# Two-step graph layer with top-p attention: slots of one row tile, PE's work interleaved by hand, proofs tested once a step

## The chip, the cores and the metric

The kernel runs on one core of a Trainium2 chip. Its engines work side by side, each through its own list of instructions in order: TensorE (PE in the profile; PEld is its weight loads), VectorE (DVE), ScalarE (ACT), GpSimd (POOL) and SyncE (SP), which here only issues transfers. The metric is device microseconds (us) of one execution of the whole program, as the median of several runs.

## The reference, cut to what matters

```python
def attention(X):                       # top-p attention, TOP_P = 0.9
    q = X @ W1.T @ W2.T                 # 64 wide
    k = X @ W3.T
    probs = softmax(q @ k.T, axis=-1)
    # per row: keep the largest entries until their sum reaches 0.9
    ...
    A = probs * mask
    return A / A.sum(-1)

h = relu(layernorm(x))                  # x is 3327 x 256
R = adj + eye; R = R / R.sum(-1)
Xf = Xa = h; Z = 0
for n in range(2):
    A = attention(Xa)
    Xf = R @ Xf
    Xa = A @ Xa
    Z = Z + Xf @ U1[n].T + Xa @ U2[n].T
out = x + layernorm(h + Z) * ln_g + ln_b
```

Everything is in 32-bit floats. The hard part is the mask: each row of 3327 exponentials has to be cut at the value where the largest ones first hold 90% of the row's sum.

## The kernel before, in words

The 3327 rows are padded to 3328, that is 26 row tiles (NT) of 128 rows. There are two functions. `guess_graph_layer` does the work with a guessed cut for every row and proves the guess; if a proof fails for any row, a flag is set, and `tile_graph_layer` (line 713) then runs `search_graph_layer`, which finds every cut by bisection. In the trace only the first one runs.

Ahead of the steps, a loop over the tiles takes the layernorm of x and calls `prep`, which makes keys and queries of a tile. Each of the two steps then runs over the row tiles, and a tile t goes through these stages:

- `weights` (from line 446): the query is projected (pq, lines 450 and 451), all 3328 logits of the tile are made on PE (pl, line 473), and ACT takes the exponentials (e, lines 477 to 482) with their sums. Then POOL works through a string of 128x1 instructions (lines 483 to 511): from the row's sum Z and the moments of its logits it guesses a threshold, column 9, and the bias column 10 for ACT.
- `first` (from line 516): ACT passes over e twice, with Relu (line 520) and Sign (line 522), and so finds the mass and the count above the guess. A string on POOL (lines 523 to 529) corrects the guess.
- `second` (from line 532): DVE passes over e once more (jv, line 536) for the mass below the corrected guess, and POOL corrects again (lines 538 to 563) and gives column 16.
- `settle` (from line 566): DVE blanks everything above column 16 (w, line 571) and sums it, finds the eight largest of each of 20 segments (cand, line 576), takes the 48 largest of these in six rounds of eight (lines 581 and 583), and finds among them the exact cut. It then cuts e in place (line 594). Seven instructions on POOL (lines 599 to 605) test whether the cut is proven, and add to the flag.
- `attend` (from line 608): PE transposes the cut e in groups of four 128x128 blocks (pt, line 614), ACT copies each group to SBUF (eT, line 616), and PE multiplies with the node values (pa, line 618). DVE takes the reciprocal of the row sum (ra, line 621), and ACT scales (xa, line 622).
- `prep` of the new values in step 0, `finish` in step 1 (from line 642): finish multiplies the four parts with U1 and U2 (pz, line 648), adds, normalises (y, lines 651 to 658) and stores (line 660). pa and pz share one PSUM buffer.
- `diffuse` (from line 625), called by `spread` (line 673): the product with the adjacency (pr, line 632), whose blocks `at` come by six transfers on SP (line 630) into three buffers. DVE adds the identity (line 638) and POOL scales (line 639).

The driver loop at the end of the function writes, for slot i: settle(i), second(i+1), attend and prep or finish of i-1, weights(i+3), first(i+2), spread(i). This is the order in which the instructions are traced. The Tile framework lays them out on each engine by itself: earlier traced ones have priority, but one that its own estimate finds ready goes ahead of one that waits. So the order on an engine need not be the traced one; in the trace, pr matmuls of spread, which is traced last, run between the groups of attend. The waits between engines come from the data.

Of the kernel before, what the change touches and what calls it, by code (L numbers as in the profile page):

```python
# [9 lines left out]
F32 = mybir.dt.float32  # L10
# [8 lines left out]
P = 128  # L19
# [304 lines left out]
def guess_graph_layer(ctx, tc, x, adj, w1t, w2t, w3t, u1t, u2t, ln_g, ln_b, out, flag):  # L324
# [9 lines left out]
    small = ctx.enter_context(tc.tile_pool(name="small", bufs=6))  # L334
# [53 lines left out]
    qm = const.tile([P, 2, 2 * DA + 1], F32, tag="qm", name="qm")  # L388
# [48 lines left out]
    def moments(step):  # L437
# [5 lines left out]
        V.tensor_copy(qm[:, step, DA:], pq[:, 0, : DA + 1])  # L443


    def weights(step, t):
# [4 lines left out]
        PE.matmul(pq[:, 1:3, :].rearrange("p a b -> p (a b)")[:, : 2 * DA + 1], qry[qp, j, :],  # L451
                  qm[qp, step, :], start=True, stop=True)
        qT = tpool.tile([P, P], F32, tag="qT", name="qT", bufs=2)
        S.copy(qT, pq[:, 0, :])
        r = {}
        mq = small.tile([P, 2], F32, tag="mq", name="mq")
        qj = small.tile([P, DA], F32, tag="qj", name="qj", bufs=1)
        pr_ = pq[:, 1:3, :].rearrange("p a b -> p (a b)")
        V.tensor_copy(mq[:, 0:1], pr_[:, 2 * DA : 2 * DA + 1])
        qs = small.tile([P, DA], F32, tag="qs", name="qs", bufs=2)  # L460
        V.tensor_copy(qs, pr_[:, :DA])
        V.scalar_tensor_tensor(qj, qs, 1.0, pr_[:, DA : 2 * DA], ALU.mult, ALU.mult,
                               accum_out=mq[:, 1:2])
        e = epool.tile([P, NP], F32, tag="e", name="e")
        za = small.tile([P, 4], F32, tag="za", name="za")
        G.memset(e[:, N:NP], 0.0)
        w = HALF * P
        for n, c in enumerate(range(0, w, 512)):
# [7 lines left out]
            if wd == 512:  # L476
                S.activation(e.rearrange("p (a n) -> p a n", a=2)[:, :, c : c + wd], pl[:, :, :wd],  # L477
                             AF.Exp, accum_out=za[:, n : n + 1])
            else:
                zb = small.tile([P, 1], F32, tag="zb", name="zb")  # L480
                S.activation(e[:, c : c + wd], pl[:, 0, :wd], AF.Exp, accum_out=zb)
                S.activation(e[:, w + c : N], pl[:, 1, : wd - 1], AF.Exp, accum_out=za[:, n : n + 1])
                G.tensor_tensor(za[:, n : n + 1], za[:, n : n + 1], zb, ALU.add)

        g = small.tile([P, 24], F32, tag="g", name="g")
        col = lambda k: g[:, k : k + 1]
        m = mq[:, 0:1]
        G.tensor_tensor(g[:, 5:7], za[:, 0:2], za[:, 2:4], ALU.add)
        G.tensor_tensor(col(0), col(5), col(6), ALU.add)
        G.tensor_tensor(col(1), col(0), pwr[:, 5:6], ALU.pow)  # L490
        G.tensor_scalar(col(1), col(1), 10.0, None, ALU.mult)
        G.tensor_scalar(col(2), m, m, mq[:, 1:2], ALU.mult, ALU.subtract)
# [261 lines left out]
```

## Time and profile before

| | |
|---|---|
| median of 3 runs | 3013.88 us (3010.37 to 3015.91) |
| the profiled execution | 3012.75 us |
| its span, from first to last instruction | 3010.9 us |
| mean granted clock of TensorE | 0.826 |
| PE busy | 2023.4 us, 67% of the span |
| POOL busy | 1538.8 us, 51% |
| DVE busy | 1188.7 us, 39% |
| ACT busy | 841.3 us, 28% |

Busy time is the time in which at least one instruction of the engine runs; matmuls are pipelined, so a busy PE is not PE at its peak. A wait is listed as: engine, tile and line that waited, then what released it, with the sum in us, the number of times and the longest. In rows in order of time stand the start, the duration, the engine, the line, the operation, out<-in, shapes and the count; in brackets the idle time before it and what ended that.

### The profile page before, as it was taken

The numbers are of one execution on the slowest core, as the hardware profiler recorded it, in microseconds if no ns is written. First come the engines' busy times: TensorE is split into PE (matmuls) and PEld (weight loads), VectorE is DVE, ScalarE is ACT, GpSimd is POOL, SyncE is SP. The second block draws the span as 40 slices with busy tenths as digits, with TensorE's granted clock in tenths as the row PEclk, the third lists the DMA queues.
The fourth block names the chain that finished last, engine by engine and source line by source line (L and its number), as shares of the span: only waits on it lengthen the run. The fifth ranks groups of instructions, "written<-read, shape, count | busy, mean of one in ns | idle before, by whom it ended". The sixth has DMA issues, their size and how long they took to land.

```text
span 3010.9 us, 28189 instructions
## 1 busy us (share of the span) xinstructions
PE 2023.4 (67%) x9055; PEld 1557.0 (52%) x9055; DVE 1188.7 (39%) x3075; ACT 841.3 (28%) x1536; POOL 1538.8 (51%) x3711
## 2 busy tenths in 40 slices
PE   7846666666766666778846567666676767576778
PEld 5534444445545454556634445455554545454566
DVE  2145544443535343442045534433433353334330
ACT  4422323223232323222332232222223222322221
POOL 4375655555454545553186655455455545554531
PEclk9968777787878888888977878887888878888889
DMA  4110000000001101111110010111011011101111
GB/s 127 56 36 28 19 23 15 19 23 23 23 20 30 36 29 37 32 37 46 38 41 21 26 31 27 31 44 31 27 36 39 26 31 40 35 26 31 40 40 38
DMA packets 58605, 102.31 MB, mean 34 GB/s; under 512 B 7249, under 2 KB 25168, under 8 KB 58448
## 3 DMA queue, kind: packets, MB, share of 16 engines
q1 hardware_dynamic: 55936, 98.85, 11.3%
q10 hardware_dynamic: 2512, 1.57, 0.2%
q8 instruction: 73, 1.20, 0.2%
q14 instruction: 84, 0.69, 0.1%
HBM read 96.99 MB, written 3.41 MB: 33 GB/s over the span
## 4 chain that ended last, share of the span: by engine, by line
POOL 43%; PE 18%; DVE 16%; ACT 11%; issue 10%; DMA 2%; SPq 0%; ACTq 0%; POOLq 0%; DVEq 0%
PE pr L632 6%; DVE w L571 6%; POOL g L552 6%; ACT ja L522 5%; DVE cand L576 4%; PE pz L648 4%; ACT ja L520 4%; POOL f L600 3%; PE pa L618 2%; DVE cand L583 2%; DVE bb L581 2%; DMA xr<-in_x 1%; POOL g L504 1%; PE pk L423 1%; PE pt L412 1%
## 5 line engine op out<-in xcount | busy, mean ns | idle before, releaser
L618 PE MATMUL pa<-xa,eT 128*128 128x257 f32 x1352 | 374.3, 434 | 246.7 <-ACT eT L616 246.7
L618 PE MATMUL pa<-x,eT 128*128 128x257 f32 x1352 | 371.0, 432 | 246.4 <-ACT eT L616 246.3
L536 DVE SCALAR_TENSOR_TENSOR jv<-e,g 128x3328 f32<-128x3328 f32 x52 | 191.7, 3686 | 754.4 <-POOL g L529 754.4
L618 PEld LDWEIGHTS pa<-xa,eT 128*128 128x128 f32 x1352 | 286.0, 218 | 322.9 <-ACT eT L616 275.3
L618 PEld LDWEIGHTS pa<-x,eT 128*128 128x128 f32 x1352 | 287.4, 218 | 318.0 <-ACT eT L616 268.7
L632 PE MATMUL pr<-xf,at 128*128 128x256 f32 x1352 | 346.7, 396 | 73.8 <-DVE xf L638 39.1
L632 PE MATMUL pr<-x,at 128*128 128x257 f32 x1352 | 371.2, 409 | 1.5 <-DMA at<-in_adj 0.9
L616 ACT COPY eT<-pt 128x512 f32<-128x512 f32 (+1 forms) x364 | 186.2, 554 | 647.1 <-PE pt L614 646.9
L571 DVE SCALAR_TENSOR_TENSOR w<-e,g 128x3328 f32<-128x3328 f32 x52 | 192.2, 3697 | 435.1 <-POOL g L563 412.3
L520 ACT ACTIVATE ja<-e,g 128x3328 uint8<-128x3328 f32 x52 | 159.5, 3067 | 703.9 <-POOL g L508 703.9
L632 PEld LDWEIGHTS pr<-xf,at 128*128 128x128 f32 x1352 | 248.4, 196 | 121.5 <-DMA at<-in_adj 41.6
L632 PEld LDWEIGHTS pr<-x,at 128*128 128x128 f32 x1352 | 256.2, 204 | 38.9 <-issue 3.8
L576 DVE MAX8 cand<-w 128x8 f32<-128x168 f32 (+1 forms) x1040 | 253.6, 317 | 1.1
L648 PE MATMUL pz<-u,xT 128*128 128x256 f32 x416 | 143.1, 506 | 149.2 <-ACT xa L622 148.8
L473 PE MATMUL pl<-k,qT 64*128 64x512 f32 (+1 forms) x832 | 196.4, 589 | 66.8 <-ACT e L477 62.2
L614 PE MATMUL pt<-ident,e 128*128 128x128 f32 x1352 | 185.8, 276 | 24.4 <-DVE e L594 13.6
L648 PEld LDWEIGHTS pz<-u,xT 128*128 128x128 f32 x416 | 106.0, 262 | 179.5 <-ACT xa L622 158.2
L594 DVE SCALAR_TENSOR_TENSOR e<-e,v 128x3328 f32<-128x3328 f32 x52 | 191.7, 3687 | 0.0
L477 ACT ACTIVATE e<-pl 128x1024 f32<-128x1024 f32 x156 | 158.6, 1020 | 98.3 <-PE pl L473 98.1
L614 PEld LDWEIGHTS pt<-ident,e 128*128 128x128 f32 x1352 | 161.4, 142 | 47.4 <-DVE e L594 14.0
L552 POOL TENSOR_SCALAR g<-g 128x1 f32<-128x1 f32 x52 | 180.7, 3476 | 5.3
L600 POOL TENSOR_SCALAR f<-v,f 128x1 f32<-128x1 f32 x52 | 172.0, 3308 | 16.0 <-DVE v L591 15.3
(154 smaller groups left out, 2490.4 us busy)
## 6 DMA issues: line engine op xcount, KB each, us to landing
at<-in_adj SPq DMA_DIRECT2D x260, 320.0 KB, 3.0
x<-in_x SPq DMA_DIRECT2D x13, 256.0 KB, 4.5
xr<-in_x SPq DMA_DIRECT2D x26, 128.0 KB, 2.2
at<-in_adj SPq DMA_DIRECT2D x52, 64.0 KB, 1.9
out<-y SPq DMA_DIRECT2D x25, 128.0 KB, 1.7
u<-in_u1t ACTq DMA_DIRECT2D x2, 256.0 KB, 6.2
u<-in_u2t ACTq DMA_DIRECT2D x2, 256.0 KB, 6.9
wk<-in_w3t ACTq DMA_DIRECT2D x2, 64.0 KB, 4.3
```

Source lines behind the costliest of these rows:

```text
L473: PE.matmul(pl[:, a, :wd], qT[p, :], keys[step][p].rearrange("p a b -> p (a b)")[:, c : c + wd], start=True, stop=True)
L520: S.activation(ja, e, AF.Relu, bias=col(10), accum_out=oa[:, 0:1])
L536: V.scalar_tensor_tensor(jv, e, col(13), e, ALU.is_lt, ALU.mult, accum_out=d1)
L552: G.tensor_scalar(col(7), c1, col(1), 14.0, ALU.mult, ALU.mult)
L571: V.scalar_tensor_tensor(w, e, col(16), e, ALU.is_lt, ALU.mult, accum_out=d2)
L576: V.max(cand[:, 8 * s : 8 * s + 8], w[:, s * SEG : min(NP, (s + 1) * SEG)])
L594: V.scalar_tensor_tensor(e, e, v[:, 1:2], e, ALU.is_ge, ALU.mult)
L600: G.tensor_scalar(f, v[:, 0:1], t, f, ALU.is_lt, ALU.add)
L614: PE.transpose(pt[:, j, :], e[:, (j0 + j) * P : (j0 + j + 1) * P], ident)
L618: PE.matmul(pa, eT[:, j, :], xa[:, j0 + j, :], start=j0 + j == 0, stop=j0 + j == NT - 1)
L632: PE.matmul(pr[:, :w], at[:, j, :], xf[:, j0 + j, :w], start=j0 + j == 0, stop=j0 + j == NT - 1)
L648: PE.matmul(pz[:, :D], xT[:, c, :], u[:, n, c, :], start=i == 0 and c == 0, stop=i == 3 and c == ND - 1)
```

## The change

The driver is rewritten by slots of one row tile, in which the pr matmuls of spread and the two passes of `first` are handed out one by one between the groups of attend. `first` and `diffuse` become generators for that. weights(i+2) is traced in slot i for weights(i+3), and spread(i+1) for spread(i). Step 0 drops `second`: `first` goes on to column 16 there. Step 0 takes five rounds of eight candidates, step 1 six as before. The tests of the proofs move out of `settle` into `prove`, once per step on DVE, from values that `settle` leaves in `rec`. The strings of POOL are reordered and shortened, the guess has a polynomial of second degree for one of fourth, and a negated column of the first moment comes from PE. In diffuse, ACT scales on the way out of PSUM and DVE adds; POOL no longer scales.

The core of the diff:

```diff
-ROUNDS = 6
-TOPK = 8 * ROUNDS
-PG = (5.74843733, -6.98979285, 0.99704953, 5.43935628, -3.98711357)
+ROUNDS = (5, 6)
+PG = (0.72168716, 3.51308980, -3.48705157)
+TOPK = 8 * max(ROUNDS)
...
-    small = ctx.enter_context(tc.tile_pool(name="small", bufs=6))
+    small = ctx.enter_context(tc.tile_pool(name="small", bufs=4))
...
+    def first(step, r):
         e, col = r["e"], r["col"]
         oa = small.tile([P, 2], F32, tag="oa", name="oa")
+        for k, f in enumerate((AF.Relu, AF.Sign)):
+            ja = scan.tile([P, NP], U8, tag="ja", name="ja")
+            S.activation(ja, e, f, bias=col(9), scale=-1.0, accum_out=oa[:, k : k + 1])
+            if k == 0:
+                yield
+
+        G.tensor_scalar(col(6), oa[:, 1:2], 0.5, NP / 2.0, ALU.mult, ALU.add)
+        G.tensor_scalar(col(5), col(6), col(9), oa[:, 0:1], ALU.mult, ALU.subtract)
+        G.tensor_scalar(col(12), col(5), col(1), 0.1, ALU.mult, ALU.max)
+        if step == 1:
+            G.tensor_scalar(col(5), col(12), 10.0, None, ALU.min)
+            G.tensor_tensor(col(5), col(5), col(11), ALU.pow)
+            G.tensor_scalar(col(13), col(5), col(9), None, ALU.mult)
+            return
+        G.tensor_scalar(col(5), col(12), -1.0, None, ALU.add)
...
+        G.tensor_tensor(col(16), col(5), col(8), ALU.add)
...
+    def prove(step):
+        v8, t, tn, Z = (rec[:, step, k, :] for k in range(4))
+        ok = small.tile([P, NT], F32, tag="cum", name="ok", bufs=1)
+        o2 = small.tile([P, NT], F32, tag="dr", name="o2", bufs=1)
+        V.tensor_tensor(ok, v8, t, ALU.is_lt)
+        V.tensor_tensor(o2, tn, t, ALU.is_lt)
...
+        V.tensor_tensor(fl, fl, f, ALU.add)
+        V.tensor_tensor(fl[:n], fl[:n], ok[:n, NT - 1 :], ALU.add)
...
+        eT = turn(0)
+        for k, j0 in enumerate(starts):
+            nxt = turn(starts[k + 1]) if k + 1 < len(starts) else None
+            fill(k)
+            for j in range(min(4, NT - j0)):
                 PE.matmul(pa, eT[:, j, :], xa[:, j0 + j, :],
                           start=j0 + j == 0, stop=j0 + j == NT - 1)
+            eT = nxt
...
             for j in range(n):
                 PE.matmul(pr[:, :w], at[:, j, :], xf[:, j0 + j, :w],
                           start=j0 + j == 0, stop=j0 + j == NT - 1)
+                if j0 + j < NT - 1:
+                    yield
...
-        V.tensor_tensor(dst, pr[:, :D], xf[:, t, :D], ALU.add)
-        G.tensor_scalar(dst, dst, rrs[:, t : t + 1], None, ALU.mult)
+        S.activation(dst, pr[:, :D], AF.Copy, scale=rr)
+        V.scalar_tensor_tensor(dst, xf[:, t, :D], rr, dst, ALU.mult, ALU.add)
...
+        for i in range(-2, NT + 1):
...
             if 0 <= i < NT:
+                settle(step, i, live[step, i])
+            meas = first(step, live[step, i + 1]) if 0 <= i + 1 < NT else iter(())
+            work = spread(step, i + 1) if 0 <= i + 1 < NT else iter(())
+
+            def fill(k):
+                run(work, (4, 4, 4, 4, 4, 3, 0)[k])
+                if k in (1, 3):
+                    next(meas, None)
+
+            if i >= 1:
+                t = i - 1
+                r = live.pop((step, t))
+                if step == 0:
+                    attend(r["e"], x0, xa1[:, t, :D], rows_of(t), fill)
+                else:
+                    xa2 = row.tile([P, D], F32, tag="xa2", name="xa2")
+                    attend(r["e"], xa1, xa2, P, fill)
+            run(meas, 3)
+            if step == 1 and 0 <= i + 1 < NT:
                 second(live[step, i + 1])
+            if 0 <= i + 2 < NT:
+                live[step, i + 2] = weights(step, i + 2)
+            run(work, NT)
             if i >= 1:
+                if step == 0:
+                    prep(1, xa1, t)
+                else:
+                    finish(t, live.pop(("f", t)), xa2)
+        prove(step)
```

More of the change, by code (lines that the diff above doesn't have):

```diff
@@ L609, in attend, with turn @@
+    def attend(e, xa, dst, n, fill):
         pa = ps_a.tile([P, D + 1], F32, tag="pa", name="pa")
-        for j0 in range(0, NT, 4):
+        starts = list(range(0, NT, 4))
+        def turn(j0):
             w = min(4, NT - j0)
@@ L674, in spread @@
         if step == 0:
[L675 to L689 removed]
+            return diffuse(x0, t, D + 1, xf1[:, t, :])
@@ L691, in guess_graph_layer, with run @@
+        live["f", t] = row.tile([P, D], F32, tag="xf2", name="xf2", bufs=3)
+        return diffuse(xf1, t, D, live["f", t])
+    def run(work, n):
+        for _ in range(n):
+            next(work, None)
     for step in range(2):
         moments(step)
-        for i in range(-3, NT + 1):
+        work = iter(())
+        for i in range(-2, NT + 1):
             if 0 <= i < NT:
-                settle(live[step, i], rows_of(i))
-            if 0 <= i + 1 < NT:
+                settle(step, i, live[step, i])
[15 more added lines that the diff above has]
+            if step == 1 and 0 <= i + 1 < NT:
```

181 lines of the change are left out of this document (75 added, 106 removed).

## The prediction, made before the changed kernel ran

> **What bounds the kernel now.** I read the page first, then stretches of steady work, the waits, one slot in order of time, and last the stretches in which TensorE (PE) is never idle.
>
> ```profile
> span 3010.9 us, 28189 instructions
> ...
> PE 2023.4 (67%) x9055; PEld 1557.0 (52%) x9055; DVE 1188.7 (39%) x3075; ACT 841.3 (28%) x1536; POOL 1538.8 (51%) x3711
> ...
> POOL 43%; PE 18%; DVE 16%; ACT 11%; issue 10%; DMA 2%; SPq 0%; ACTq 0%; POOLq 0%; DVEq 0%
> ```
>
> The second row is busy time, the third the chain that ended last. No engine is full: POOL, half busy, holds 43% of the chain, PE only 18%. So the kernel waits on POOL's strings of 128x1 instructions, while PE has a third of the span to spare.
>
> ```profile
> 405.20:1397.00 991.80, 651.75 (x2858) 501.29 (x2858) 416.52 (x1069) 284.54 (x501) 513.68 (x1266) 0.81 0.09 26
> 1832.50:2901.90 1069.40, 719.29 (x3120) 552.73 (x3120) 414.41 (x1046) 280.30 (x486) 545.17 (x1278) 0.83 0.11 33
> 2925.00:3000.00 75.00, 71.03 (x359) 59.42 (x357) 5.43 (x17) 13.90 (x32) 8.55 (x14) 1.00 0.14 40
> ```
>
> ```profile
> 405.00:1396.90 991.90, 69.87 (x19) 0.81 0.09 26
> 1832.00:2901.00 1069.00, 66.18 (x18) 0.83 0.11 33
> ```
>
> The columns of the first fence are PE, weight loads, DVE, ACT, POOL, granted clock; the second counts L594, the cut of e, once per row tile. So a slot (one row tile) lasts 991.8/19 = 52.2 us in step 0 and 1069.4/18 = 59.4 in step 1, and PE is busy 34.3 and 40.0 us of it.
>
> ```profile
> ACT ja L520 <- POOL g L508: 222.2, 19, 13.5
> ...
> PE pa L618 <- ACT eT L616: 200.5, 20, 12.6
> ACT xa L622 <- DVE ra L621: 183.1, 19, 11.6
> ```
>
> ```profile
> PE pa L618 <- ACT eT L616: 182.4, 18, 12.0
> ...
> PE pz L648 <- ACT xa L622: 130.0, 18, 8.3
> ```
>
> These are waits in the two steady stretches. ACT stands for the Relu sum (L520) until POOL gives its bias; the copies eT that PE needs are queued behind it. PE loses 10.6 us a slot (200.5/19) in step 0 and 10.1 in step 1, where finish costs another 7.2.
>
> ```profile
> 999.25 3.69 DVE L536 SCALAR_TENSOR_TENSOR jv<-e,g 128x3328 f32<-128x3328 f32 x1 [19.67 <-POOL g L529]
> ...
> 1011.11 3.68 DVE L571 SCALAR_TENSOR_TENSOR w<-e,g 128x3328 f32<-128x3328 f32 x1 [8.16 <-POOL g L563]
> ...
> 1026.95 3.83 POOL L600 TENSOR_SCALAR f<-v,f 128x1 f32<-128x1 f32 x1 [0.33 <-DVE v L591]
> ...
> 1032.90 0.19 POOL L483 TENSOR_TENSOR za<-za,zb 128x1 f32<-128x1 f32 x1
> ...
> 1041.23 3.07 ACT L520 ACTIVATE ja<-e,g 128x3328 uint8<-128x3328 f32 x1 [11.95 <-POOL g L508]
> ...
> 1048.21 0.20 ACT L522 ACTIVATION_READ_ACCUMULATOR ja<-e,g 128x1 f32 x1
> ...
> 1051.49 3.68 DVE L536 SCALAR_TENSOR_TENSOR jv<-e,g 128x3328 f32<-128x3328 f32 x1 [18.81 <-POOL g L529]
> ...
> 1051.56 3.75 POOL L552 TENSOR_SCALAR g<-g 128x1 f32<-128x1 f32 x1
> ```
>
> This is the loop of step 0, 52.24 us from jv to jv: second 11.9 (999.25 to 1011.11), cut and candidates 15.8 (to 1026.95), proof flags 5.95, weights' string on POOL 8.3, Relu and Sign 7.2, first 3.1. Nothing of the next tile overlaps, because POOL reaches weights' string only behind the flags of the tile before.
>
> **The change part by part.**
>
> *Second and its jv leave step 0; flags leave both steps.* The loop loses 11.86 + 5.95 and one of six candidate rounds, priced below at 0.72: 52.24 falls to 33.7 even if no order changed. PE's own work is about as long, so PE is next.
>
> ```profile
> L581 DVE MAX8 bb<-cand 128x8 f32<-128x160 f32 x312 | 101.4, 325 | 7.7
> ...
> L583 DVE MATCH_REPLACE8 cand<-bb,cand 128x160 f32<-128x160 f32 x260 | 80.2, 308 | 0.0
> ...
> L583 DVE MATCH_VALUE_LOAD cand<-bb,cand 128x8 f32 x260 | 23.6, 91 | 7.5
> ```
>
> A round is 0.325 + 0.308 + 0.091 = 0.72 us. The new prove is about a dozen 128x26 DVE instructions a step; at most those rows' 0.33 each, 4 us, at least nothing, since they need only the cut of the last tile and PE still has a slot of attend to do. I take nothing; without that cover it is 4 us a step.
>
> *POOL's strings.* Weights' string runs 22 instructions in 8.33 us (L483 to the Relu), 0.38 each with the gaps. Ten of them now lie between the last exponential and the bias: 3.8 us; the others stand before or behind. First has 13 in step 0 (4.9) and 6 in step 1 (2.3); second has 22 for 23 and stays at 7.9 after its jv. The scale of diffuse leaves POOL for an ACT copy and a small DVE instruction; ACT is 15 us busy a slot (284.54/19), so these are covered. Four buffers of small tiles for six cost nothing, since a tile's lie over three slots. POOL falls to some 36 x 0.38 = 14 us a slot in step 0, from 27.0.
>
> *PE's floor.*
>
> ```profile
> 1426.39 1.04 PE L614 MATMUL pt<-ident,e 128*128 128x128 f32 x8
> ...
> 1447.27 6.79 PE L632 MATMUL pr<-x,at 128*128 128x257 f32 x30
> 1453.90 1.04 PE L614 MATMUL pt<-ident,e 128*128 128x128 f32 x8
> ...
> 1477.21 0.38 PE L450 MATMUL pq<-qry,w2d 64*128 64x128 f32 x2
> ...
> 1481.40 0.38 PE L450 MATMUL pq<-qry,w2d 64*128 64x128 f32 x2
> ```
>
> ```profile
> 2945.30 1.04 PE L614 MATMUL pt<-ident,e 128*128 128x128 f32 x8
> ...
> 2975.68 1.04 PE L614 MATMUL pt<-ident,e 128*128 128x128 f32 x8
> ```
>
> At the end of each step PE runs without a gap. Attend, spread and prep of a tile take 27.5 us, attend, spread and finish 30.4; weights takes 4.2. Dense slots are therefore 31.7 and 34.6 us, today's busy time 34.3 and 40.0. The difference is the clock:
>
> ```profile
> 2872.36 6.52 PE L618 MATMUL pa<-xa,eT 128*128 128x257 f32 x16 [10.59 <-ACT eT L616]
> ...
> 2880.03 3.71 PE L618 MATMUL pa<-xa,eT 128*128 128x257 f32 x16
> ```
>
> The same 16 matmuls take 6.52 us after 10.6 us of idling and 3.71 a few us later; granted clock is 0.81 to 0.83 in the steady stretches, 1.00 in the dense one. I take the middle, 33.0 and 37.3, since some gaps will stay. The Trainium skill (TensorE: Matmul & The Clock Gate, "Part 1: The HAM clock gate") says that the array falls to half its clock after an idle window of about 3.4 us and comes back after a busy one. By that rule, with gaps all shorter than this, slots would be 1.3 and 2.7 us shorter and the sum about 2150. The pair of rows agrees.
>
> *Waits that stay or come.*
>
> ```profile
> 2997.97 0.42 DVE L651 TENSOR_TENSOR y<-pz,x 128x256 f32<-128x256 f32 x1 [1.44 <-PE pz L648]
> ```
>
> The interleaving puts four pr matmuls between one eT copy and the next attend matmuls, and Relu and Sign at two fixed places. By the row above four (eight records) are 8 x 0.226 = 1.8 us, with the 16 records of pa half of 3.7 and the transposes 0.5: some 4.2 us of PE cover against 3.07 + 0.2 of Relu. I cost that at nothing; bare, it is up to 3.3 us twice a slot. What PE will wait for, taken at half of one 3.68 us DVE instruction each: (a) 1.8 for the reciprocal behind attend, queued on DVE among the next tile's settle (today 183.1 us of ACT's waiting in step 0 is of this kind); (b) 1.8 for a late Relu bias, when POOL's string is caught by a DVE pass; (c) in step 1, 2.2 for y (0.42 by its row, plus 1.8), since pz and the next pa share one PSUM buffer; (d) in step 1, 1.5 for adjacency blocks, as now:
>
> ```profile
> 2857.61 2.86 PE L632 MATMUL pr<-xf,at 128*128 128x256 f32 x12 [1.53 <-DMA at<-in_adj]
> ```
>
> On SP the six at loads now stand one slot earlier and ahead of the store of out, which waits for finish; the xr load and the store come behind them. Bounds of (a) to (d): nothing, and 3.7, 3.7, 4.1 and 3.5. The diffuse copy on ACT waits for the last pr matmul, with prep's copies queued behind it; PE is then at that work anyhow, so nothing, at most 1.
>
> For (b) the row is L552: 3.75 us beside a DVE pass over e, against 0.38 for its neighbours. The Trainium skill (GPSIMD Engine Reference, "1. Specifications") says that GpSimd shares its SBUF interfaces with VectorE and contends with DVE instructions of two SBUF inputs. That speaks against the change, since the cuts w and e stay: with a full hold each slot the sum would be about 2350. The trace agrees with the rule.
>
> *Slots.* Step 0: 33.0 + 1.8 + 1.8 = 36.6. Step 1: 37.3 + 1.8 + 1.8 + 2.2 + 1.5 = 44.6. The other loop in step 1, cut and candidates 17.8, jv 3.7, second 7.9, is 29.4 us and hidden by PE; with weights' whole string between, 37.7, still hidden.
>
> *Sum.*
>
> ```profile
> 112.02 0.37 PE L450 MATMUL pq<-qry,w2d 64*128 64x128 f32 x1
> ```
>
> ```profile
> 118.84 0.21 ACT L482 ACTIVATION_READ_ACCUMULATOR e<-pl 128x1 f32 x1
> ...
> 2646.68 3.69 DVE L571 SCALAR_TENSOR_TENSOR w<-e,g 128x3328 f32<-128x3328 f32 x1 [8.16 <-POOL g L563]
> ...
> 2660.83 3.68 DVE L594 SCALAR_TENSOR_TENSOR e<-e,v 128x3328 f32<-128x3328 f32 x1
> ...
> 2996.75 1.13 PE L648 MATMUL pz<-u,xT 128*128 128x256 f32 x4 [0.40 <-ACT xT L414]
> ```
>
> Step 0 starts at 112.0. Its first tile needs exponentials 7.0, string 3.8, Relu and Sign 2 x 3.27 = 6.5, first 4.9, settle 17.1 (17.8, from 2646.68 to 2664.5, less a round): 151.3. Then 26 slots of 36.6, less 4.2 for the last three, which have no weights, and 11.8 (52 x 0.226) for the last two without spread: I take 36.2. Step 0 ends at 1066.7. Step 1: 7.0 + 3.8 + 6.5 + 2.3 + 3.7 + 7.9 + 17.8 = 49.0, then 26 x 44.6 - 36.2: 2239.1. From the last matmul to the end is 13.0 today (2997.9 to 3010.9), and 1.85 lie around the span (3012.75). That is 2254 us, made against the profiled 3012.75, which is 1.1 below the median of 3013.88.
>
> **The rivals.** (1) *Floor reached* (below 2060): all waits hidden and full clock, 151.3 + 26 x 31.7 - 36.2 + 49.0 + 26 x 34.6 - 36.2 + 14.9 = 1867. For it: the gapless rows. Against: they come when DVE and POOL have no settle or weights to do. (2) *The order is not what is written* (2460 to 2900): the build lays instructions out by its own estimate of when they are ready. The pr matmuls traced last in a slot run today inside attend, so hand interleaving may add little, and the Relu may be lifted ahead of the eT copies again. If PE keeps 10.6 and 10.1 us of that wait, slots are 44.9 and 50.1 and the time 2254 + 26 x (8.3 + 5.5) = 2613. It decides once the bias comes later than the first eT copy is due. Against: flags are gone and the string is 3.8 for 8.3. (3) *Slower*: a proof fails. Step 0 now rests on a threshold guessed from one sum and on 40 candidates; one row without proof runs the search (line 713) behind everything: 27 halvings x 52 tiles x one ACT pass of 3.07 + 0.2 us is 4591, together about 6845 us. It decides at the first row whose cut lies more than 40 candidates from the guess. No line of the search stands in the trace of before, so all proofs hold there with 48 candidates; nothing in the profile shows how near they come to failing. (4) *No gain within 0.2%*, about what a measurement of this kernel can tell from no change: only if POOL's shorter loop were no part of the bound, against the 43%.
>
> **How the numbers follow.** Forecast (2060 to 2460) 0.59; floor 0.12; written order undone 0.22; slower 0.05; same 0.02. The time is the forecast's, 2254. Waits of nothing to double move it by 26 x 10.9 = 283 either way; the range, 2000 to 2700, covers most of that and reaches part of the way into both rivals; the outer parts of (1) and (2), and (3) and (4), are left out. Faster 0.93, same 0.02, slower 0.05.
>
> **What would show it.** Right: the cut of e comes every 36 to 38 us in step 0 and 43 to 46 in step 1; PE above 85% busy with granted clock near 0.9; POOL gone from the head of the chain and PE there; the eT wait of PE under 3 us a slot; no jv in step 0. Wrong: eT waits of 10 us, a reciprocal or y that holds PE for more than 4 us a slot, pr waiting for its buffer or at in the midst of attend, or instructions of the search in the trace.

## The result and the profile after

The changed kernel takes 2560.95 us (median of 4 runs, 2557.2 to 2566.17) where the kernel before took 3014.89 beside it. The ratio is 0.8498, with a 95% interval of 0.8479 to 0.8516. The forecast was 2254, in a range of 2000 to 2700, so the sign and the range held, and the size was off by 307 us: two fifths of the forecast gain of 760 did not come.

The page of the kernel after, first lines, busy time and the chain that ended last:

```profile
span 2555.4 us, 26919 instructions
...
PE 1945.5 (76%) x9055; PEld 1524.5 (60%) x9055; DVE 1100.5 (43%) x2969; ACT 866.6 (34%) x1588; POOL 900.7 (35%) x2541
...
DVE 33%; POOL 29%; PE 14%; ACT 13%; issue 9%; DMA 0%; ACTq 0%; POOLq 0%; DVEq 0%
```

POOL has shrunk from 1538.8 us to 900.7, as the forecast had said. But PE isn't full, and it doesn't head the chain, as the forecast had it: DVE does, an engine that is busy 43% of the time. An engine that heads the chain while it is mostly idle suggests a loop of waits, and the rows below show one.

The two steady stretches of the kernel after (PE, weight loads, DVE, ACT, POOL, granted clock), and waits of the whole execution (total us, times, longest):

```profile
507.60:999.10 491.50, 416.30 (x1945) 326.96 (x1945) 218.66 (x625) 188.16 (x336) 136.64 (x456) 0.92 0.15 42
1425.80:2383.80 958.00, 682.12 (x3132) 539.53 (x3132) 419.74 (x1045) 288.42 (x504) 386.21 (x990) 0.85 0.13 38
```

```profile
ACT xa L652 <- DVE ra L651: 437.1, 52, 13.5
...
PE pl L476 <- ACT e L480: 321.8, 51, 12.8
...
ACT ja L520 <- POOL g L503: 237.4, 52, 13.6
...
PE pa L647 <- ACT eT L639: 11.1, 5, 7.3
```

The stretches hold 12 and 18 slots, so a slot takes 491.5/12 = 41.0 us in step 0 and 958/18 = 53.2 in step 1, where the forecast had 36.6 and 44.6. PE is busy 34.7 and 37.9 of it. The 10.6 and 10.1 us a slot that PE waited for the eT copies before are gone: 11.1 us in all. In their place ACT waits for `ra`, the reciprocal behind attend, once per tile, 8.4 us on average (437.1/52), and PE waits for the exponentials.

One slot of step 0 in order of time (start, duration, engine, line) shows who waits for whom:

```profile
698.48 3.69 DVE L585 SCALAR_TENSOR_TENSOR w<-e,g 128x3328 f32<-128x3328 f32 x1 [7.57 <-POOL g L542]
...
710.03 2.77 PE L647 MATMUL pa<-x,eT 128*128 128x257 f32 x12
...
711.76 3.69 DVE L605 SCALAR_TENSOR_TENSOR e<-e,rec 128x3328 f32<-128x3328 f32 x1
...
715.71 0.16 DVE L651 RECIPROCAL ra<-pa 128x1 f32<-128x1 f32 x1
715.90 0.48 ACT L652 ACTIVATE xa<-pa,ra 128x256 f32<-128x256 f32 x1 [6.55 <-DVE ra L651]
...
716.58 4.92 PE L476 MATMUL pl<-k,qT 64*128 64x512 f32 x16 [2.51 <-ACT qT L459]
...
722.62 0.19 POOL L494 TENSOR_TENSOR g<-za 128x2 f32<-128x2 f32 x1 [3.52 <-ACT e L483]
...
727.96 3.07 ACT L520 ACTIVATE ja<-e,g 128x3328 uint8<-128x3328 f32 x1 [4.40 <-POOL g L503]
...
731.58 0.20 ACT L433 COPY kr<-pk 128x64 f32<-128x64 f32 x1
731.69 3.07 ACT L520 ACTIVATE ja<-e,g 128x3328 uint8<-128x3328 f32 x1
...
731.89 0.45 PE L435 MATMUL pg<-kr 128*64 128x65 f32 x2 [4.01 <-issue]
...
734.75 1.05 ACT L639 COPY eT<-pt 128x512 f32<-128x512 f32 x2
734.94 0.19 POOL L524 TENSOR_SCALAR g<-oa 128x1 f32<-128x1 f32 x1 [2.44 <-ACT ja L520]
...
740.15 3.69 DVE L585 SCALAR_TENSOR_TENSOR w<-e,g 128x3328 f32<-128x3328 f32 x1 [7.56 <-POOL g L542]
```

Read it as one loop from w to w, 41.67 us: settle, to the end of the cut, 16.97 (698.48 to 715.45); `ra`, xa, the query's copy and the exponentials 7.17 (to 722.62); weights' string 5.34 (to 727.96); Relu and Sign 6.98 (to 734.94); first's string 5.21 (to 740.15). The driver is written so that weights, first and settle of one slot belong to three different tiles. On the engines they belong to one tile and run one behind the other. What closes the loop is the place of `ra`: attend had ended by 712.8, but its reciprocal stands on DVE behind a whole settle, xa waits for it on ACT, and the next tile's exponentials are queued on ACT behind xa. The next tile's moments (L462 to L465), which weights' string needs, stand behind the settle too. Relu and Sign lie ahead of all eT copies of the next attend (734.75), and the small copies of prep lie behind Relu: PE has been idle for 4.0 us when it starts pg (L435), whose input kr is copied just before (L433).

Step 1, the same view, from cut to cut:

```profile
2011.63 3.68 DVE L605 SCALAR_TENSOR_TENSOR e<-e,rec 128x3328 f32<-128x3328 f32 x1
...
2015.47 0.47 ACT L652 ACTIVATE xa<-pa,ra 128x256 f32<-128x256 f32 x1 [12.72 <-DVE ra L651]
...
2020.58 0.19 POOL L494 TENSOR_TENSOR g<-za 128x2 f32<-128x2 f32 x1 [2.76 <-ACT e L483]
...
2025.70 3.07 ACT L520 ACTIVATE ja<-e,g 128x3328 uint8<-128x3328 f32 x1 [3.29 <-POOL g L503]
...
2033.38 0.19 POOL L524 TENSOR_SCALAR g<-oa 128x1 f32<-128x1 f32 x1
...
2037.53 3.68 DVE L549 SCALAR_TENSOR_TENSOR jv<-e,g 128x3328 f32<-128x3328 f32 x1 [3.80 <-POOL g L530]
2037.59 3.75 POOL L564 TENSOR_SCALAR g<-g 128x1 f32<-128x1 f32 x1
...
2050.01 3.69 DVE L585 SCALAR_TENSOR_TENSOR w<-e,g 128x3328 f32<-128x3328 f32 x1 [8.79 <-POOL g L574]
...
2064.11 3.68 DVE L605 SCALAR_TENSOR_TENSOR e<-e,rec 128x3328 f32<-128x3328 f32 x1
...
2067.71 0.16 DVE L651 RECIPROCAL ra<-pa 128x1 f32<-128x1 f32 x1
```

The loop is 52.48 us: cut 3.7, reciprocal to exponentials 5.3, weights' string 5.1, Relu and Sign 7.7, first 4.2, jv and second 12.5, w and candidates 14.1. Attend had ended at 2053.5, and its reciprocal came at 2067.71.

### The profile page after: what moved, and what is told of

The parts are those of the page before. It is cut to its first block, busy times and chain, and to the rows that moved or that the text cites. A ratio compares the mean times of both kernels' runs of the same rounds, so it can differ in the third digit from the quotient of the medians.

```text
span 2555.4 us, 26919 instructions
## 1 busy us (share of the span) xinstructions
PE 1945.5 (76%) x9055; PEld 1524.5 (60%) x9055; DVE 1100.5 (43%) x2969; ACT 866.6 (34%) x1588; POOL 900.7 (35%) x2541
## 4 chain that ended last, share of the span: by engine, by line
DVE 33%; POOL 29%; PE 14%; ACT 13%; issue 9%; DMA 0%; ACTq 0%; POOLq 0%; DVEq 0%
DVE cand L589 9%; DVE w L585 7%; ACT ja L520 7%; DVE e L605 7%; PE pl L476 4%; ACT e L480 4%; POOL g L564 4%; DVE cand L596 3%; DVE bb L594 3%; PE pz L681 3%; PE pa L647 2%; PE pr L662 2%; POOL g L503 1%; POOL g L499 1%; POOL g L507 1%
## 5 line engine op out<-in xcount | busy, mean ns | idle before, releaser
L476 PE MATMUL pl<-k,qT 64*128 64x512 f32 (+1 forms) x832 | 226.0, 672 | 357.4 <-ACT e L480 321.8
L520 ACT ACTIVATE ja<-e,g 128x3328 uint8<-128x3328 f32 x104 | 319.3, 3070 | 237.5 <-POOL g L503 237.4
L476 PEld LDWEIGHTS pl<-k,qT 64*128 64x128 f32 x832 | 87.8, 232 | 494.1 <-ACT e L480 400.8
L647 PE MATMUL pa<-x,eT 128*128 128x257 f32 x1352 | 326.6, 386 | 10.6 <-ACT eT L639 10.6
L647 PE MATMUL pa<-xa,eT 128*128 128x257 f32 x1352 | 319.5, 380 | 0.5 <-ACT eT L639 0.5
L662 PEld LDWEIGHTS pr<-x,at 128*128 128x128 f32 x1352 | 267.9, 211 | 46.1 <-issue 4.2
L647 PEld LDWEIGHTS pa<-x,eT 128*128 128x128 f32 x1352 | 254.8, 193 | 46.9 <-ACT eT L639 11.9
L647 PEld LDWEIGHTS pa<-xa,eT 128*128 128x128 f32 x1352 | 255.1, 190 | 37.3 <-ACT eT L639 1.2
L637 PE MATMUL pt<-ident,e 128*128 128x128 f32 x1352 | 227.5, 301 | 4.7 <-DVE e L605 4.7
L637 PEld LDWEIGHTS pt<-ident,e 128*128 128x128 f32 x1352 | 189.0, 157 | 41.3 <-DVE e L605 5.1
L489 POOL TENSOR_SCALAR g<-mq 128x1 f32<-128x1 f32 x52 | 17.8, 342 | 510.0 <-DVE rec L607 335.5
L605 DVE SCALAR_TENSOR_TENSOR e<-e,rec 128x3328 f32<-128x3328 f32 x52 | 191.5, 3682 | 4.6
L652 ACT ACTIVATE xa<-pa,ra 128x256 f32<-128x256 f32 (+1 forms) x52 | 24.7, 475 | 437.1 <-DVE ra L651 437.1
```

The costliest lines, as they stand in the source:

```text
L476: PE.matmul(pl[:, a, :wd], qT[p, :], keys[step][p].rearrange("p a b -> p (a b)")[:, c : c + wd], start=True, stop=True)
L520: S.activation(ja, e, f, bias=col(9), scale=-1.0, accum_out=oa[:, k : k + 1])
L605: V.scalar_tensor_tensor(e, e, at(1), e, ALU.is_ge, ALU.mult)
L637: PE.transpose(pt[:, j, :], e[:, (j0 + j) * P : (j0 + j + 1) * P], ident)
L647: PE.matmul(pa, eT[:, j, :], xa[:, j0 + j, :], start=j0 + j == 0, stop=j0 + j == NT - 1)
L662: PE.matmul(pr[:, :w], at[:, j, :], xf[:, j0 + j, :w], start=j0 + j == 0, stop=j0 + j == NT - 1)
```

## The experiments

Three theories stand against each other. **A**: the loop just shown, closed by the order on DVE. **B**: the forecast's, that PE's own work and a few short waits set the slot. **C**: the second rival, that Relu and Sign, lifted ahead of the eT copies, are the cost. The table collects all runs (each time a median; the ratio is to the kernel before on the same chip; slots are the steady distance from cut to cut; e1 and e14 leave half of the adjacency product out, so their output isn't the layer's).

| run | us | ratio, 95% interval | slot, step 0 | slot, step 1 |
|---|---|---|---|---|
| after | 2560.95 | 0.8479 to 0.8516 | 41.0 | 53.2 |
| e1, half of the spread | 2378.95 | 0.7885 to 0.7912 | 37.4 | 48.7 |
| e2, w behind the moments | 2289.52 | 0.7587 to 0.7612 | 39.8 | 42.6 |
| e3, order of before | 2653.94 | 0.8792 to 0.8822 | 45.1 | 54.6 |
| e4, second back | 2693.21 | 0.8926 to 0.8978 | 46.4 | 53.1 |
| e5, Relu behind the copies | 2345.45 | 0.7768 to 0.7794 | 39.3 | 46.0 |
| e6, e2 and e5 together | 2171.76 | 0.7196 to 0.7220 | 33.4 | 44.4 |
| e7, reciprocal off DVE | 2504.45 | 0.8293 to 0.8321 | 40.9 | 51.2 |
| e8, cut twice | 2639.71 | 0.8744 to 0.8774 | 43.3 | 54.6 |
| e11, e6 and y over ACT | 2080.49 | 0.6892 to 0.6915 | 33.4 | 40.9 |
| e12, e6 and second back | 2380.38 | 0.7887 to 0.7913 | 41.0 | 44.4 |
| e13, e6 and cut twice | 2184.82 | 0.7241 to 0.7265 | 33.4 | 44.4 |
| e14, e6 and half of the spread | 1927.01 | 0.6385 to 0.6406 | 26.8 | 40.4 |

### What the order and the work are worth apart (e3, e4)

e3 keeps the work of the kernel after (strings, five and six rounds, proofs once a step, one step's second sum less) and writes it in the driver order of before, with nothing interleaved.

```diff
-        for i in range(-2, NT + 1):
+        for i in range(-3, NT + 1):
...
-            meas = first(step, live[step, i + 1]) if 0 <= i + 1 < NT else iter(())
-            work = spread(step, i + 1) if 0 <= i + 1 < NT else iter(())
...
+            if 0 <= i + 3 < NT:
+                live[step, i + 3] = weights(step, i + 3)
+            if 0 <= i + 2 < NT:
+                run(first(step, live[step, i + 2]), 3)
+            if 0 <= i < NT:
+                run(spread(step, i), NT)
```

> The work of the changed kernel (no second sum in step 0, shorter strings, proofs once a step) written in the order of the kernel before: settle, second, attend with prep or finish, weights three ahead, first two ahead, spread last, nothing interleaved by hand. Theory A: the ring is still there and takes prep or finish in as well, since weights stand behind them on PE: 4 us more a slot in step 0 and 5 to 6 in step 1, 2780 to 2850 us. If the gain is all from the removed work: 2550 to 2580. If the order makes all of it: near 3000.

It took 2653.94, below A's range and above that of the removed work alone. Of A's slots, step 0 came (4.1 us more, for 4), step 1 didn't (1.4 more, for 5 to 6). So of the 454 us that the change gains, the work it removes, with what else differs inside the functions, is worth about 358 in the old order (3012.0 to 2653.9), and the new order and the interleaving some 93 more (2653.9 to 2561). Order by hand brought little here, as the second rival had feared.

e4 keeps the second sum in step 0 as well.

```diff
-            if step == 1 and 0 <= i + 1 < NT:
+            if 0 <= i + 1 < NT:
                 second(live[step, i + 1])
```

> The changed kernel with the second sum kept in step 0 as well (both steps guess alike). Theory A: its pass of 3.7 us and its string of 7.9 lie on the ring, step 0 slots go from 41.7 to about 53, in all 2561 + 26 x 11.6, about 2860 us. Theory B: PE hides most of it, 2561 to 2650. Theory C: as B, since it does not touch the Relu.

It took 2693.21: 132 more, where A had said some 300. The steady slot of step 0 grew by 5.4 us, not by 11.7. Its trace says why: the query's copy and the logits' first two matmuls came to stand ahead of xa on ACT and PE, so that only 2.8 us of exponentials lie behind `ra` (xa 844.39, weights' string 847.22) in place of 6.7, and first's string is some seven instructions shorter when second follows. 41.0 + 11.7 - 3.9 - 2.7 = 46.1 for the measured 46.4. So the loop is there, but an edit of the work also moves the layout, and the price of an edit isn't only its own time.

### The loop opened by an order alone (e2)

Nothing is added or removed. The settle's first pass is only held on DVE behind the moments of the next tile (L462 to L465, of which `last` is L465), which in the kernel after ran behind the whole settle.

```diff
+    def queued(step, t):
+        return tc.issue_after(live[step, t]["last"].ins) if t < NT else nullcontext()
...
-        V.scalar_tensor_tensor(w, e, col(16), e, ALU.is_lt, ALU.mult, accum_out=d2)
+        with queued(step, t + 1):
+            V.scalar_tensor_tensor(w, e, col(16), e, ALU.is_lt, ALU.mult, accum_out=d2)
```

> The changed kernel with one order added: the first pass of settle (w) of a tile is queued on VectorE behind the logit moments (qj) of the next tile. No instruction is added. Theory A: the ring of 41.7 us in step 0 and 53 us in step 1 then spans two tiles and stops binding; slots fall to PE's work and waits, 36 to 39 and 44 to 47, in all 2230 to 2400 us. Theory B: PE is the bound already, 2540 to 2580. Theory C: the Relu still stands ahead of the eT copies, 2530 to 2580.

It took 2289.52, 271 us less than the kernel after with the same instructions. The order on DVE is now reciprocal, moments, w (rows of step 0; and POOL's first instruction of weights' string beside w):

```profile
732.25 0.17 DVE L655 RECIPROCAL ra<-pa 128x1 f32<-128x1 f32 x1 [16.23 <-PE pa L651]
...
733.52 0.22 DVE L465 SCALAR_TENSOR_TENSOR qj<-qs,pq 128x64 f32<-128x64 f32 x1
...
733.66 3.68 DVE L589 SCALAR_TENSOR_TENSOR w<-e,g 128x3328 f32<-128x3328 f32 x1
733.86 3.70 POOL L489 TENSOR_SCALAR g<-mq 128x1 f32<-128x1 f32 x1 [5.40 <-DVE qj L465]
```

Now DVE waits for PE at the reciprocal (16.23 us), and PE heads the chain:

```profile
PE 58%; POOL 21%; issue 10%; ACT 7%; DVE 3%; DMA 0%; ACTq 0%; POOLq 0%; DVEq 0%
```

That shows A: what held the kernel after was the place of a few short DVE instructions behind a settle. B falls, since PE's work is unchanged, and so does C as the whole cause, since Relu still stands ahead of the eT copies here. Most of the gain is step 1's, whose slot falls by 10.6 us. Step 0's falls by 1.2 only (41.0 to 39.8), because a second loop, shown under e7, is nearly as long there.

### Less PE, more DVE, and the reciprocal alone, on the kernel after (e1, e8, e7)

e1 leaves out every second adjacency block.

```diff
             for j in range(n):
-                PE.matmul(pr[:, :w], at[:, j, :], xf[:, j0 + j, :w],
-                          start=j0 + j == 0, stop=j0 + j == NT - 1)
+                if (j0 + j) % 2 == 0:
+                    PE.matmul(pr[:, :w], at[:, j, :], xf[:, j0 + j, :w],
+                              start=j0 + j == 0, stop=j0 + j == NT - 2)
```

> The changed kernel with every second adjacency block left out of the product in spread (half of R's columns are missing from Xf). PE loses 26 of 52 matmuls of 0.226 us a slot, 5.9 us. Theory A (a ring of waits through VectorE: the reciprocal behind attend and the logit moments stand on VectorE behind the whole settle of a later tile, and the exponentials of the next tile wait for them): PE is not the bound, time within 1% of the changed kernel, 2535 to 2585 us. Theory B (the forecast: PE's work and a few waits on top make the slot): 2561 - 52 x 5.9, about 2255. Theory C (the Relu pass ahead of the eT copies stops PE): between, 2400 to 2500, since PE has less to do before and after that stop.

It took 2378.95, which lies between what B and C gave and farthest from A's. PE fell to 70% of the span, so PE's load is no bound there, yet the slots shrank by 3.6 and 4.5 us. The trace shows another layout: in step 0 the first exponential stands ahead of xa on ACT, and some 4 us of the loop with it; in step 1 the reciprocal came to stand among the candidates, ahead of the cut (ra 2070.96, cut 2075.82), and 4.9 us of the loop with it. An experiment that takes work away changes what the build lays out, so this run tells nothing cleanly.

e8 does the cut twice; the second pass leaves e as it is.

```diff
         V.scalar_tensor_tensor(e, e, at(1), e, ALU.is_ge, ALU.mult)
+        V.scalar_tensor_tensor(e, e, at(1), e, ALU.is_ge, ALU.mult)
```

> The kernel after with the cut of e done twice in every settle (the second pass leaves e as it is): 3.68 us more of VectorE a slot, nothing else. Theory A (VectorE's settle lies on a loop that sets the slot): every slot grows by all of it, 2561 + 52 x 3.7 = 2753, 2735 to 2770. Theories B and C (TensorE, or its wait for the eT copies, sets the slot, and VectorE, 43% busy, has room): 2561 to 2610.

It took 2639.71, 79 us more: over B's bound, and short of A's. The slots grew by 2.3 and 1.4 us where the pass takes 3.68. In step 0 the logits are made before the reciprocal here, and stand by while ACT waits:

```profile
742.28 1.99 PE L476 MATMUL pl<-k,qT 64*128 64x512 f32 x8
...
748.79 0.16 DVE L652 RECIPROCAL ra<-pa 128x1 f32<-128x1 f32 x1
748.87 0.14 DVE L462 COPY mq<-pq 128x2 f32<-128x2 f32 x1
```

From xa to weights' string it is 5.1 us now (748.98 to 754.08) in place of 6.72. In step 1 the second pass lies behind the reciprocal, and the exponentials run beside it; only the moments wait for it. So DVE's settle is on the loop, as A says, and A's count of it was too simple.

e7 takes the reciprocal off DVE and leaves the moments where they are.

```diff
-        V.reciprocal(ra, pa[:, D : D + 1])
+        S.copy(ra, pa[:, D : D + 1])
+        G.tensor_tensor(ra, ra, pwr[:, 5:6], ALU.pow)
```

> The kernel after with attend's reciprocal taken off VectorE: ScalarE copies the row sums from PSUM, GpSimd raises them to -1, ScalarE scales as before. The result is the same. The moments still stand behind the settle on VectorE. This is one part of theory A alone. A: in step 0 the attend has ended 3 us before its reciprocal runs, and the exponentials behind the scaling start that much earlier; in step 1 the exponentials leave the loop (about 5 us) but the moments behind the cut now hold the whole weights' string of 22 instructions (8.3 us for the 10.4 us from reciprocal to bias now), so 2 us a slot: 26 x 3 + 26 x 2 = 130 less, 2430, 2380 to 2490. The forecast's own price (1.8 us a slot for a reciprocal that TensorE waits for, and nothing queued behind it): 26 x 2 x 1.8 = 94 less at most, 2467; these two lie too close to be told apart by the time alone, and are told by the rows: by A the cuts stay locked to the moments. Theory C: nothing, 2540 to 2570.

It took 2504.45, outside A's range. Step 1 did what A said: 2.0 us a slot less (51.2), locked to the moments. Step 0 gained nothing (40.9), and its rows show a second loop that had been hidden:

```profile
693.04 1.06 ACT L639 COPY eT<-pt 128x512 f32<-128x512 f32 x2
...
711.33 2.77 PE L647 MATMUL pa<-x,eT 128*128 128x257 f32 x12
...
715.84 0.48 ACT L653 ACTIVATE xa<-pa,ra 128x256 f32<-128x256 f32 x1 [1.54 <-POOL ra L652]
...
726.66 3.07 ACT L520 ACTIVATE ja<-e,g 128x3328 uint8<-128x3328 f32 x1 [4.37 <-POOL g L503]
...
733.45 1.05 ACT L639 COPY eT<-pt 128x512 f32<-128x512 f32 x2
```

From eT copy to eT copy: attend 21.1 us (693.04 to 714.1), reciprocal 1.7, xa, query and exponentials 5.7, weights' string 5.2, Relu and Sign 6.8 (to 733.45), 40.4 in all. This loop goes through PE and doesn't touch the settle; it is closed by Relu and Sign ahead of the eT copies of the next attend, and is only half a microsecond shorter than the first. Some 1.5 us of it are e7's own: its reciprocal takes 1.7 us over ACT and POOL, where the one on DVE takes 0.16. That is C, as a loop and not as PE's wait for eT: PE does matmuls of the spread while the copies wait, and is idle elsewhere.

### Both loops (e5, e6)

e5 holds Relu and Sign behind the eT copies after which they are written; e6 has this and e2's order.

```diff
-            S.copy(eT[:, :w, :], pt[:, :w, :])
+            made[0] = S.copy(eT[:, :w, :], pt[:, :w, :])
...
-            S.activation(ja, e, f, bias=col(9), scale=-1.0, accum_out=oa[:, k : k + 1])
+            with tc.issue_after(made[0].ins) if made[0] else nullcontext():
+                S.activation(ja, e, f, bias=col(9), scale=-1.0, accum_out=oa[:, k : k + 1])
```

> The kernel after, with one kind of order added: Relu and Sign of a tile stay on ScalarE behind the third and fifth eT copy of the attend in which they are written, where the build had laid them ahead of all of them. No work changes. In the order that is laid out, VectorE then has the reciprocal and the next tile's logit moments directly behind the w pass, where the kernel after has them behind the whole settle. Theory A (reciprocal and moments behind the settle close a loop of one tile): the loop is opened by another handle than in the run that queued w behind the moments, so near that run: 2290, 2230 to 2370. Theory C (rival 2: Relu ahead of the eT copies is itself the cost, and it holds TensorE): 2254, 2200 to 2330. Theory B (nothing in the order, TensorE's own work and clock set the 2561): 2530 to 2590. A and C aren't told apart by this run alone; the next one does that.

> Both orders together: w behind the next tile's moments, and Relu and Sign behind the eT copies. Theory A: the loop is open already with the first order alone (2289.5), so the second brings little: 2260 to 2310. Theory C: Relu still stands ahead of the eT copies in the run with the first order alone; there the copies of prep and the first eT copy wait behind Relu and Sign, and TensorE stands idle 4.0 us a slot in step 0 and less in step 1. Taking Relu out of their way gives that back: 26 x 4 and some of step 1, so 2130 to 2210.

e5 took 2345.45, inside A's range and just over C's. With Relu later, first and w come later, and the reciprocal is laid out behind w, in step 0 also behind candidates, no longer behind the cut: in step 0 it still comes some 5 us late (attend ends at 715.7, ra 720.48), in step 1 10 us. So the one order opens the loop of Relu and, by these rows, a part of the other.

e6 took 2171.76, inside C's range and below A's. Both loops are real, and in e2 the second one was what was left. The steady stretches of e6:

```profile
412.70:879.90 467.20, 446.68 (x2269) 352.62 (x2268) 250.77 (x728) 221.56 (x393) 201.24 (x532) 1.00 0.18 52
1188.70:2031.40 842.70, 716.16 (x3307) 565.40 (x3307) 451.90 (x1103) 301.29 (x532) 533.80 (x1046) 0.92 0.15 45
```

In step 0, 14 slots, PE is busy 446.68 of 467.2 us at a granted clock of 1.00: 31.9 us a slot, for the dense 31.7 of the prediction. This is the state the forecast described, and it is reached by order alone. In step 1 PE's longest wait is the one for y:

```profile
PE pa L654 <- DVE y L691: 115.4, 19, 6.1
```

A's number came in two of the eight runs up to here, e2 and e5, and neither of the others did better. The cause rests on e2 and e6, in which nothing but an order changes and the rows show the loops open; where work was added or taken away (e1, e4, e7, e8), the layout moved with it.

### What is left, and what it hides (e11 to e14)

e11 frees the PSUM buffer by an ACT copy.

```diff
-        V.tensor_tensor(y, pz[:, :D], x0[:, t, :D], ALU.add)
+        S.copy(y, pz[:, :D])
+        V.tensor_tensor(y, y, x0[:, t, :D], ALU.add)
```

> Both orders (2171.8), and finish's sum y in two parts: ScalarE copies pz out of PSUM, VectorE then adds the rows of x to the copy. The result is the same. In step 1 of the run with both orders, TensorE waits 6.1 us a slot for y, which stands on VectorE among the settle, because pz and the next attend share one PSUM buffer. Theory: that wait is what step 1 still loses; the copy takes about 0.5 us and leaves 0.6 of it, so 26 x 5.5 = 143 less: 2029, 2015 to 2060. Rival (the loop of Relu, first, jv, second and w on GpSimd and VectorE bounds step 1, and TensorE would wait there next): 2120 to 2172.

It took 2080.49: less by 91 where 143 was expected. The slot fell from 44.4 to 40.9, and the y wait is gone, but another wait stands in its place (step 1, 1150 to 2000 us):

```profile
PE pr L669 <- DMA at<-in_adj: 80.4, 21, 4.6
```

The adjacency blocks hold PE 3.8 us a slot; in the kernel after they held it 0.2 us in all. The rival, a loop over POOL and DVE, is not what took over. This is the fastest version that does the whole work: 0.81 of the kernel after (0.6903/0.8498).

e12, e13 and e14 put second into step 0, the double cut and the halved spread on e6, with the edits shown above.

> Both orders (2171.8), and the second sum kept in step 0 as well. The pair on the kernel after gave 132 us for that work (2693.2 against 2561). Theory (with the loops opened, TensorE bounds step 0, 95.6% busy at a granted clock of 1.00, and VectorE's and GpSimd's extra 11.7 us a slot lie beside it): 2172 to 2200. Rival (the work has a price of its own, in whatever order): 2280 to 2310.

It took 2380.38, more than either expected: 209 us for work that cost 132 in the kernel after. Step 0 is bounded by PE no more. Second makes w late, and the two short DVE instructions that make diffuse's scale (L676, L677) now stand behind it and the first candidates, with the only pr buffer waiting for them (500 to 1000 us, and rows of one slot):

```profile
PE pr L669 <- ACT xf L678: 71.3, 12, 5.9
```

```profile
732.42 3.69 DVE L592 SCALAR_TENSOR_TENSOR w<-e,g 128x3328 f32<-128x3328 f32 x1 [5.21 <-POOL g L577]
...
738.51 0.14 DVE L676 TENSOR_SCALAR rs<-pr 128x1 f32<-128x1 f32 x1
...
738.81 0.14 DVE L677 RECIPROCAL rrs<-rs 128x1 f32<-128x1 f32 x1
```

It is the mechanism of `ra` at another place: an instruction of 0.14 us for which PE waits, behind a long pass. The granted clock there is 0.92. PE was busy 418.91 of these 500 us, that is 34.4 us of a slot of 41.0, for 31.9 of 33.4 in e6: of the 7.6 us more a slot, some 2.5 are the same matmuls at a lower clock and some 5.1 are idle time, an estimate from these two stretches.

> Both orders (2171.8), and the cut of e done twice (the second pass leaves e as it is), as in the run on the kernel after, where it cost 79 us. Theory (VectorE's settle is on no loop any more in step 0; in step 1 it lies ahead of or behind y, for which TensorE waits): 2172 to 2190, or up to 26 x 3.7 = 96 more if y comes to stand behind the second pass. Rival (VectorE still on a loop): 2250 to 2360.

It took 2184.82: 13 more, within the theory's range, and the slots stayed at 33.4 and 44.4. The pass that cost 79 us in the kernel after is covered once the loops are open.

> Both orders (2171.8), and every second adjacency block left out of the matmuls (the output isn't the reference's): 5.9 us less of TensorE a slot. Theory (TensorE bounds step 0): there 26 x 5.9 = 153 less at most, some of it met by the next limit; in step 1, where TensorE waits for y on VectorE, anything from nothing to as much: 1880 to 2070. Rival (another loop of about the same length holds step 0): 2130 to 2172.

It took 1927.01, within the theory's range. Step 0's slot fell by 6.6 us to 26.8 in the second half of the step, at least all of the 5.9 removed: PE bounds that step. Step 1 fell by 4.0; PE waits 8.1 us a slot for y there.

## Why the prediction was right in sign and wrong in size

**What held.** The removed work left as costed: no jv in step 0, POOL down to 11.4 us a slot there (136.64/12; forecast 14). No instruction of the search stands in the trace, so the third rival didn't come. PE's eT wait fell from about 10 us a slot to 11.1 in all, though not in the forecast way: Relu and Sign weren't spread between the copies, and some 4 us a slot of step 0 are idle at pg instead. The tail from the last matmul of pz to the end is 13.2 us (2542.2 to 2555.4), forecast 13.0. PE's floor was right: 31.9 us at full clock in e6 for 31.7.

But the mechanism wasn't the forecast's. By its own signs, cuts were to come every 36 to 38 and 43 to 46 us (41.0 and 53.2 came), and PE was to be over 85% busy (76%) and at the head of the chain (DVE is). That the time lies in the range is owed to the width of the range, 700 us, and so in part to luck.

**Where the 303 us of span are.** The forecast had the first cut of step 1 start at 1066.7 + 49.0 - 3.7 = 1112.0 and the span end at 2252.2; measured are 1242.7 and 2555.4. So 131 us were lost up to there, 172 behind it. In step 0, 19 of them lie ahead of the first cut (166.8 for 147.6, mostly because the second tile's w was laid between the first one's candidates and its cut, and DVE stood 9.8 us for it). Another 85 lie from there to the step's last matmul of prep (1170.4 for 1066.7): the last 17 distances from cut to cut are 4.4 us longer each, two whole attends follow the last cut, for which the forecast had left no time, and a quicker start, with several tiles in flight, gives 35 back. The last 27 lie before step 1's first cut (72.3 for 45.3). In step 1 the slots are 8.6 longer, less a shorter start, since the first three cuts come within 41 us; and 52 us lie between the last cut and the last matmul, where the forecast left 12.

**The step that failed** is the sentence on the other loop: "The other loop in step 1, cut and candidates 17.8, jv 3.7, second 7.9, is 29.4 us and hidden by PE; with weights' whole string between, 37.7, still hidden." The loop has more in it. Exponentials behind the reciprocal (5.3), Relu and Sign (7.7) and first (4.2) are on it too: 37.7 + 17.2 = 54.9, which is longer than the forecast's slot of 44.6, and near the measured 53.2. In step 0 the text had the sum, "52.24 falls to 33.7 even if no order changed", and took it for no bound because PE's work is as long. It lacked two things that before ran beside other work, as rows of the kernel before show:

```profile
1025.31 1.02 ACT L477 ACTIVATE e<-pl 128x1024 f32<-128x1024 f32 x1 [1.44 <-PE pl L473]
...
1026.93 3.68 DVE L594 SCALAR_TENSOR_TENSOR e<-e,v 128x3328 f32<-128x3328 f32 x1
```

The next tile's exponentials ran beside the candidates, though the forecast says that nothing of the next tile overlaps; now 7.2 us from cut to last exponential are on the loop. And the cut of e ran beside the flags: the 15.8 us that the forecast calls cut and candidates hold w and candidates alone, and end (1026.95) where the cut begins. With the flags gone, the cut's 3.7 us are on the loop, while 1.8 us of short DVE work for other tiles no longer lie among the candidates: 1.9 more. First's new string is 2.1 longer and weights' 3.0 shorter. 33.7 + 7.2 + 1.9 + 2.1 - 3.0 - 0.2 (Relu and Sign) is the 41.7 of the slot shown.

**Term (a)**, the reciprocal among the next tile's settle, had the right place and the wrong size and victim. It was priced at half a DVE pass, 1.8 us, and as a wait of PE. Measured is 8.4 us a tile, beyond its bound of 3.7, because a whole settle can stand ahead; and the price isn't PE's wait but what stands behind xa on ACT.

**Terms (b), (c), (d).** (b) POOL is held beside DVE passes: 3.75 us at L564, one of each slot in step 1, but jv's own end was awaited there anyhow, so it cost little. (c) could be seen in e6 alone: 6.1 us a slot for y, over its upper bound of 4.1, for a like reason as (a), a place behind candidates (y starts at 1628.89 in a slot whose last matmul of pz ended at 1621.6). (d) came out in e11, 3.8 us, above the 1.5 taken and its bound of 3.5. In the kernel after, (c) and (d) hid behind the loop.

**The second rival** had the right layout and nearly the right time (2613 for 2561), by another way than it said. Relu is lifted ahead of the eT copies, as it foresaw, but PE doesn't wait for eT; what it closes is a second loop, 40.4 us long in e7, which e6 priced at 118 us once the first loop was open (2289.5 to 2171.8). That its time was near is partly chance: in step 1 the slot is 53.2 where it said 50.1, in step 0 41.0 where it said 44.9.

**On the clock**, the forecast took 33.0 us for step 0's PE work between the busy and the dense values; with the loops open it is 31.9 and the granted clock 1.00. The Trainium skill (TensorE: Matmul & The Clock Gate, "Part 1: The HAM clock gate") gives the full clock after a busy window and takes it back after an idle one. E6's row, 1.00 with PE 95.6% busy, agrees with it.

## What to carry to other kernels

Before counting what a bounding engine does, write down every loop that leads from a tile's long pass back to the next tile's, with all that stands in the queues between, and ask for each short instruction what may be laid ahead of it on its engine. A driver order by hand didn't fix that here: three tiles written to be in flight ended as one. An order edge at the one place where a long pass overtakes a short instruction that others wait for was worth more here (e2, 271 us; with e5's, 389) than the whole of the interleaving (93).

## What the runs showed of the hardware

The same 9055 matmuls of PE are busy for 1945.5 us in the kernel after, 1873.3 in e6 and 1841.8 in e11, and the granted clock is higher where the idle gaps are gone (0.92 in step 0 of the kernel after, 1.00 in e6's): taking away waits also shortened the work.

One POOL instruction of 128x1, weights' first, as groups of the kernel after and of e2 (total busy us, mean ns, idle before):

```profile
L489 POOL TENSOR_SCALAR g<-mq 128x1 f32<-128x1 f32 x52 | 17.8, 342 | 510.0 <-DVE rec L607 335.5
```

```profile
L489 POOL TENSOR_SCALAR g<-mq 128x1 f32<-128x1 f32 x52 | 172.3, 3313 | 184.3 <-DVE qj L465 170.8
```

It takes ten times as long where it is issued beside w, a DVE pass with e at both inputs. The Trainium skill (GPSIMD Engine Reference, "1. Specifications") names contention with DVE instructions of two SBUF inputs, and the rows agree. In the slot of e2 shown above, all but about 1 us of that is hidden: the exponentials end at 738.56, and the string goes on with their sums at 739.55.
